# Reordering loads, splits and GpSimd's sums in a graph-attention and top-p diffusion kernel

## Chip, cores and metric

The kernel runs on one core of a Trainium2 chip. A core has five instruction queues that run beside each other: TensorE (PE, matrix products), VectorE (DVE), ScalarE (ACT), GpSimd (POOL) and SyncE (SP, which here only starts transfers). The metric is the time of one execution on the device in microseconds (us).

## What is computed

Two layers over N = 4096 nodes with D = 256 features, each with a layer norm and a relu ahead of it and the input added behind it. The first is a graph attention with 4 heads. The second runs two steps: in each, a softmax over all nodes is cut to the smallest set of largest probabilities that reaches 0.9 of the sum, and used as one neighbour matrix; a normalised adjacency is the other. Cut to what matters:

```python
# layer 0
h   = relu(layernorm(x))
e   = leaky_relu(src[:, :, None] + dst.T[None])       # src, dst: h @ W, then a
out = einsum('nhm,mhd->nhd', softmax(where(adj > 0, e, -9e15)), h @ W)
x   = x + layernorm(out) * gamma + beta
# layer 1
X   = relu(layernorm(x));  R = adj + I;  R = R / R.sum(-1)
Xf = Xa = X;  Z = 0
for n in range(2):
    p  = softmax((Xa @ W1.T @ W2.T) @ (Xa @ W3.T).T)
    A  = p * (p is among the largest that reach 0.9);  A = A / A.sum(-1)
    Xf = R @ Xf
    Xa = A @ Xa
    Z  = Z + Xf @ U1[n].T + Xa @ U2[n].T
x   = x + layernorm(X + Z) * ln_g + ln_b
```

## The kernel before

Nodes are cut into NB = 32 blocks of P = 128. The stages follow each other: a prologue (features of layer 0), layer 0's attention in 16 passes, the first graph hop (R @ Xf), attention step 0, a "join" (second graph hop, with projections for step 1 between its products), attention step 1, and a tail. Except in layer 0's passes the order on each engine is the order in which the program calls its functions (`manual_schedule`); there a scheduler places instructions within the order of dependences. [...]

**Prologue.** SP loads X (block 0, blocks 1 to 3, then four at a time), ScalarE's queue starts the loads of a_r (L198) and of the weights wx in two halves (L200). VectorE makes two columns per head out of wx and a_r (L545, L547), and each block is normalised, turned and multiplied.

**Layer 0.** A pass k is a group of 8 blocks of rows and one head; 16 pairs p of column blocks run through it. VectorE makes masks m (L375, L376), TensorE multiplies (L395). Work that belongs to an earlier pass is put into a list `later`, from which one piece is taken for each pair. Lifted sums (L578) add beta to X on GpSimd in the passes of head 0. For the first hop, `source`, `split` (L450 on ScalarE, L451 on VectorE: a row block in two parts, high and low), `edge` (load of an adjacency strip `ar`, or `aru` for every fifth) and `own` (L602: the identity added to it) prepare the first strips.

**Hops.** `hops` goes through strips n: source, edge, split, own, then the products L615. `drained` copies four sums out (L626), ScalarE and VectorE taking two each. Between step 0 and step 1, Xa is loaded back into X in eight loads, one at each sixth half step.

**Attention.** A block b has three parts: logits and exponentials two or three blocks ahead (L720, L903), the search for its threshold, and `attend`, which turns its kept probabilities (L1080, copied out by L1082) and multiplies them with X (L1088) in eight groups g of four. At the end of `attend`, L1098 multiplies by U1 and L1102 on ScalarE writes the result into xf. The search needs sums from ScalarE (L910); `first_step` on GpSimd makes of them a first limit c3 in 17 small instructions (L927 to L953); `third_probe` (L971) on VectorE uses it on the whole row, then eight-maxima (L989, L996) give the threshold, and `masked` (L1014) clears what is below.

`chosen_kept(b)` puts these in order for each block, together with the last layer norm, which only step 1 has:

- `gathered(b-1)`, GpSimd: part + v, x1 + ln_b, part + xf (L1106 to L1108). The last needs L1102.
- `finish(b-2)`, VectorE: adds the scaled sum (L1269), mean and variance (L149, L150).
- `finish_scale(b-2)`, GpSimd: rs and nmr (L1276, L1277, L1280).
- `normal(b-2)`, ScalarE: part times rs plus nmr (L1284). It comes last in `chosen_kept`, so on ScalarE it stands right behind L1102 of the block before and ahead of L903 of the next.
- `polished(b-3)`, GpSimd: times ln_g, plus x1 (L1288, L1289), and the store (L1290, SP).

The first three blocks of a step get their `first_step` in the stage before it.

**Repair.** Rows whose threshold wasn't settled are counted (`questioned`, up to L1168 on VectorE; `counted`, two matmuls L870), and a branch (L1256) behind the last block redoes blocks where there are any. `looked` does the count, `number` reads it into registers of all engines.

Of the kernel before, what the change touches and what calls it, by code (L numbers as in the profile page):

```python
# [56 lines left out]
def gat_then_top_p_diffusion(  # L57
# [104 lines left out]
    with tc.tile_pool(name="l0", bufs=1) as l0, tc.tile_pool(name="l0s", bufs=2) as l0s, tc.tile_pool(name="l0o", bufs=1) as l0o:  # L162
# [26 lines left out]
        with tc.manual_schedule(engines=every | {ET.SP}):  # L189
# [5 lines left out]
                nc.sync.dma_start(X[:, ts(g, 4), :], x[ts(g, 4 * P), :].rearrange("(b p) d -> p b d", p=P))  # L195

            nc.sync.dma_start(X[:, 0, :], x[:P, :])
            nc.scalar.dma_start(a_r, bass.AP(tensor=a.tensor, offset=a.offset, ap=[[0, P], [1, 2 * HD]]))  # L198
            for k in range(KC):
                nc.scalar.dma_start(wx[:, k, :D], w[ts(k, P), :])  # L200
            nc.sync.dma_start(X[:, 1:4, :], x[P:4 * P, :].rearrange("(b p) d -> p b d", p=P))
            for g in range(1, NB // 4):
                block_rows(g)
# [195 lines left out]
        def evacuate(k):  # L399
            ig, h = passes[k]  # L400
            acc = shared[k].acc
            if h == 0:
                out_rows[ig] = l0o.tile([P, G0, D], F32, name="o")
            st = l0o.tile([P, 4, 2 * H * (W3 + 1) // 2], F32, name="st").rearrange("p a b -> p (a b)")
            st = st[:, :G0 * 2 * W3].rearrange("p (i t k d) -> p i t k d", i=G0, t=2, k=3)
            for i in range(G0):
                b = ig * G0 + i
                one, two = (st[:, i, t].rearrange("p k d -> p (k d)") for t in range(2))
                nc.scalar.activation(two, acc[i][:, 1, :W3], AF.Copy, scale=e_c[1][:, h, b:b + 1])
                if h == 0:  # L410
                    nc.vector.reduce_sum(rinv[:, b:b + 1], acc[i][:, :, W3], axis=AX.X)
                nc.vector.scalar_tensor_tensor(one, acc[i][:, 0, :W3], e_c[0][:, h, b:b + 1], two, ALU.mult, ALU.add)

            def three():
                for n in (1, 2):
                    nc.vector.tensor_tensor(st[:, :, 0, 0], st[:, :, 0, 0], st[:, :, 0, n], ALU.add)

            def divided():
                rden = small.tile([P, G0], F32, name="rden")
                nc.vector.reciprocal(rden, st[:, :, 0, 0, HD])  # L420
                nc.vector.tensor_mul(out_rows[ig][:, :, ts(h, HD)], st[:, :, 0, 0, :HD],
                                     rden[:, :, None].to_broadcast([P, G0, HD]))
                if h == 0:
                    rs = rinv[:, ts(ig, G0)]
                    nc.vector.tensor_scalar(rs, rs, 1.0, None, ALU.add)
                    nc.vector.reciprocal(rs, rs)
            return [three, divided] + (closing(ig) if h == H - 1 else [])

        PASSES = NB // G0
        S = SimpleNamespace(spare=None)  # L430
# [15 lines left out]
        def split(A, n):  # L446
            while A.parted < min(n, len(order)):
                src = A.src[A.parted]
                hl = rp.tile([P, 2, D], F32R, name="hl", bufs=5)
                nc.scalar.copy(hl[:, 0, :], src)  # L450
                nc.vector.tensor_tensor(hl[:, 1, :], src, hl[:, 0, :].bitcast(F32), ALU.subtract)  # L451
                A.hl[A.parted] = hl
                A.parted += 1

        hop1 = hop_of(0)

        def closing(ig):
            o = out_rows[ig]
            mv = l0s.tile([P, G0, nc.vector.BN_AGGR_DIM], F32, name="mv8")
            scales = []  # L460

            def stats(i0):
                for i in range(i0, i0 + 2):
                    moments_of(mv[:, i, :], o[:, i, :])
                if i0 == G0 - 2:
                    scales.extend(steps(mv, G0, l0s))

            def close(i):
                b = ig * G0 + i
                xb = X[:, b, :]  # L470
                ob = l0s.tile([P, D], F32, name="ob")
                nc.scalar.activation(ob, o[:, i, :], AF.Identity, scale=scales[0][:, i:i + 1], bias=scales[1][:, i:i + 1])
                nc.vector.tensor_mul(ob, ob, gamma_r)
                nc.vector.tensor_add(xb, xb, ob)
                nc.sync.dma_start(x1_d[b], xb)
                moments_of(mv[:, i, :], xb)
                if i == G0 - 1:
                    steps(mv, G0, l0s, x_rs[:, ts(ig, G0)], x_nmr[:, ts(ig, G0)])

            def relu(i0):  # L480
                for b in range(ig * G0 + i0, ig * G0 + i0 + 2):
                    nc.scalar.activation(X[:, b, :], X[:, b, :], AF.Relu, scale=x_rs[:, b:b + 1], bias=x_nmr[:, b:b + 1])
                if ig == 0 and i0 < LOOK + 1:
                    for b in range(i0, min(i0 + 2, LOOK + 1)):
                        source(hop1, b)
                        split(hop1, b + 1)
            return [lambda i=i: stats(i) for i in range(0, G0, 2)] + [lambda i=i: close(i) for i in range(G0)] \
                + [lambda i=i: relu(i) for i in range(0, G0, 2)]

# [50 lines left out]
        with tc.manual_schedule(engines=every):  # L540
# [22 lines left out]
            for n, (k, p) in enumerate(todo):  # L563
# [9 lines left out]
                    products(k, p, ms.pop(n))  # L573
                if n in rest:
                    rest[n]()
                if k % H == 0 and 2 < p < PAIRS - 1 and lifted:
                    b = lifted.pop(0)
                    nc.gpsimd.tensor_tensor(X[:, b, :], X[:, b, :], beta_r, ALU.add)  # L578
                if 1 < p < PAIRS - 3 and later:
# [3 lines left out]
        passing.close()  # L583
        ps2 = ctx.enter_context(tc.tile_pool(name="ps2b", bufs=2, space=PSUM))
        ps1 = ctx.enter_context(tc.tile_pool(name="ps1b", bufs=2, space=PSUM))
        def edge(A, n):
            if n in A.ar or n >= len(order):
                return
            p, j = order[n]
            if S.spare is not None and n % 5 == 4:  # L590
                ar = S.spare.tile([P, G0 * P], F32R, name="aru", tag="u")
            else:
                ar = rp.tile([P, G0 * P], F32R, name="ar", bufs=4)
            nc.sync.dma_start(ar.bitcast(F32), adj_d[p, :, j, :].bitcast(F32))
            A.ar[n] = ar

        def own(A, n):
            while A.owned < min(n, len(order)):
                p, j = order[A.owned]
                if j // G0 == p:  # L600
                    block_ = A.ar[A.owned][:, ts(j % G0, P)]
                    nc.vector.tensor_tensor(block_, block_.bitcast(F32), ident, ALU.add)  # L602
                A.owned += 1

        def graph_products(A, m, s, halves=(0, 1)):
            j = order[m][1]
            if j == 0 and s == 0:
# [10 lines left out]
        def drained(hop, p, acc):  # L618
# [2 lines left out]
            room = S.big if last else S.l1e.tile([P, N], F32, name="stage", tag="e1")  # L621
            out_ = room[:, :N // 2].rearrange("p (c s b i) -> p c s b i", c=2, s=KC, b=4)
            rows_ = room[:, ds(N // 2, N // 2)].rearrange("p (b d) -> p b d", b=G0)
            for c in (1, 0):
                for s in range(KC):
                    (nc.vector.tensor_copy if s else nc.scalar.copy)(out_[:, c, s].rearrange("p b i -> p (b i)"), acc[c][s])  # L626

            def stored():
                for c in range(2):
# [25 lines left out]
        def hops(A):  # L655

            turned = []
            for n in range(A.begun, len(order) + LOOK + 1):
                for i in range(3 if n == A.begun else 1):
                    source(A, n + 2 - (2 - i if n == A.begun else 0))  # L660
                edge(A, n)
# [677 lines left out]
    for n in range(STEPS):  # L1339
# [4 lines left out]
        with tc.manual_schedule(engines=every):  # L1344
# [1 line left out]
            filling, picking = fills(n, G, found, blocks), picks(n, found, blocks)  # L1346
            done = 0 if n else NB - G0 - LOOK
            for i, _ in enumerate(pieces, 2 * done):
                if n > 0 and i % 6 == 5 and i // 6 < NB // 4:
                    g = i // 6  # L1350
                    nc.sync.dma_start(cur[:, ts(g, 4), :], xa_d[ts(g, 4)].rearrange("b p d -> p b d"))
                if (n == 0 or i > 10) and i // 2 % NB != NB - 2:
# [11 lines left out]
            def chosen_kept(b):  # L1364

                r = blocks[b]
                if not hasattr(r, "kept"):
                    candidates(r, found)
                if b > 2:
                    polished(blocks.pop(b - 3))  # L1370
                if b + 1 < NB and not hasattr(blocks[b + 1], "thirded"):
                    third_probe(blocks[b + 1])
                if b > 1:
                    finish(blocks[b - 2])
                    finish_scale(blocks[b - 2])
                if b + 2 < NB and not hasattr(blocks[b + 2], "stepped"):
                    first_step(blocks[b + 2])
                if 0 < b < NB - 1:
                    gathered(blocks[b - 1])
                if not hasattr(r, "kept"):  # L1380
                    masked(r)
                if 1 < b < NB - 1:
# [12 lines left out]
            def beginning():  # L1395
                normal(blocks[NB - 3])
                gathered(blocks[NB - 2])
                finish(blocks[NB - 2])
                finish_scale(blocks[NB - 2])
                R.count = number(R, R.undone)  # L1400

            beside = {NB - 2: {5: last_chosen, 6: looked}, 0: dict(zip((0, 1, 3, 5, 6), S.turned))}
            for b in range(NB - 1):
                chosen_kept(b)
                if b + AHEAD < NB:
# [6 lines left out]
                polished(blocks[NB - 3])  # L1412
                finish_rows(blocks[NB - 2])

            beside = {0: beginning, 3: earlier}
            if n + 1 < STEPS:
                second = hop_of(n + 1)
                beside.update({1: both_weights, 2: lambda: begin(second, 4), 5: lambda: split(second, 2), 6: lambda: (split(second, 4), own(second, 4))})
            attend(r, cur, None, beside)
            for m in range(second.begun if n + 1 < STEPS else 0):  # L1420
                for s in range(KC):
# [37 lines left out]
```

## Time and profile before

| | |
|---|---|
| median of three runs | 2875.74 us (2874.88 to 2879.38) |
| the profiled execution | 2872.68 us, span 2870.9 us |
| busy: TensorE, VectorE, ScalarE, GpSimd | 2798.5, 2169.1, 1919.1, 867.1 us |
| mean granted TensorE clock | 0.994 |
| layer 0's passes | some 89 to 797 us |
| first hop | to 1120 us |
| attention step 0, with its last block | to 1806 us |
| join | to 2165 us |
| attention step 1, tail | to 2845 us, to 2871 us |

The profile comes from one execution. A line of a timeline gives start and duration in us, engine, line of the program, operation, output and inputs with their shapes, and in brackets how long the engine had been idle and what released it. A line of waits gives who waited for what: us in total, times, the longest. A line of a stretch gives its ends and length, then busy time (and instructions) of PE, PE's weight loads, DVE, ACT and POOL, granted clock, share of the DMA engines and GB/s.

### The profile page before, as it was taken

How to read it: one execution, taken by the hardware profiler on the slowest of the kernel's cores; microseconds unless marked ns; L12 is line 12 of the kernel's file. 1: busy time of each engine (PE TensorE's matmuls, PEld its weight loads, DVE VectorE, ACT ScalarE, POOL GpSimd, SP SyncE). 2: the span in 40 equal slices, each digit the busy share in tenths (PEclk: the TensorE clock that was granted, in tenths of full speed). 3: DMA queues.
4: the chain of work that ended last, by engine and by line, in shares of the span. 5: the costliest groups of instructions: out<-in, count | busy, mean ns of one | idle time of the engine just before them, and what ended most of it. 6: DMA issues, size and time to landing. Idle time of an engine off the chain costs nothing. (4 is left out here: it accounts for less than half of the span.)

```text
span 2870.9 us, 51480 instructions
## 1 busy us (share of the span) xinstructions
PE 2798.5 (97%) x18777; PEld 2440.2 (85%) x18777; DVE 2169.1 (76%) x5069; ACT 1919.1 (67%) x3065; POOL 867.1 (30%) x1811
## 2 busy tenths in 40 slices
PE   5899999999999999999999999999999999999998
PEld 4899999999987788888888888667878888888887
DVE  8867878678654385888888887343574999999996
ACT  7876887779633646788777884232627778877882
POOL 6501211110000121322332221000204766666564
PEclk9999999999999999999999999999999999999999
DMA  8969587696366783000000001667991111111100
GB/s 193 243 229 222 186 232 186 242 194 226 141 227 199 237 296 104 20 20 20 24 23 20 20 20 48 217 205 234 326 349 49 31 34 39 31 31 31 41 29 25
DMA packets 190394, 376.48 MB, mean 131 GB/s; under 512 B 18224, under 2 KB 143152, under 8 KB 186032
## 3 DMA queue, kind: packets, MB, share of 16 engines
q1 hardware_dynamic: 146832, 275.05, 28.9%
q0 software_dynamic: 21504, 83.89, 12.3%
q10 hardware_dynamic: 21792, 14.11, 1.5%
q8 instruction: 152, 2.49, 0.3%
q14 instruction: 114, 0.93, 0.1%
HBM read 305.55 MB, written 113.57 MB: 146 GB/s over the span
## 5 line engine op out<-in xcount | busy, mean ns | idle before, releaser
L1088 PE MATMUL acc<-X,eT 128*128 128x256 f32 x4096 | 973.8, 383 | 3.4 <-ACT eT L1082 2.8
L1088 PEld LDWEIGHTS acc<-X,eT 128*128 128x128 f32 x4096 | 739.9, 191 | 110.5 <-ACT eT L1082 31.4
L395 PE MATMUL acc<-ut,m 128*128 128x195 bf16 (+1 forms) x8192 | 699.5, 247 | 7.0 <-DVE m L376 4.9
L395 PEld LDWEIGHTS <-m 128*128 128x128 fp8e4 x8192 | 696.1, 96 | 10.3 <-DVE m L376 6.1
L369 ACT ACTIVATE g<-sr,d_big 128x1024 uint8<-128x1024 f32 x448 | 472.8, 1136 | 6.4 <-DVE m L375 6.3
L903 ACT ACTIVATE e<-mm,nm 128x1024 f32<-128x1024 f32 x256 | 286.1, 1117 | 201.5 <-PE mm L720 197.8
L1082 ACT COPY eT<-tp 128x512 f32<-128x512 f32 x512 | 296.4, 580 | 89.5 <-PE tp L1080 89.2
L989 DVE MAX8 cand<-big 128x8 f32<-128x228 f32 (+1 forms) x1152 | 348.3, 380 | 0.0
L615 PE MATMUL mm<-ar,hl 128*128 128x512 f32 x844 | 342.7, 409 | 5.5 <-DMA ar<-adj_d 1.6
L971 DVE SCALAR_TENSOR_TENSOR big<-e,c 128x4096 f32<-128x4096 f32 x58 | 261.9, 4516 | 97.9 <-POOL c L956 67.1
L615 PE MATMUL acc<-ar,hl 128*128 128x512 f32 x844 | 329.2, 393 | 0.4 <-DVE ar L602 0.4
L927 POOL TENSOR_TENSOR sums<-sums 128x2 f32<-128x2 f32 x64 | 12.8, 200 | 1033.4 <-ACT void L910 1033.4
L1080 PE MATMUL tp<-ident,e 128*128 128x128 f32 x2048 | 306.3, 273 | 0.8 <-DVE e L1014 0.8
L1080 PEld LDWEIGHTS tp<-ident,e 128*128 128x128 f32 x2048 | 255.0, 141 | 60.2 <-PE acc L1098 1.2
L1014 DVE SCALAR_TENSOR_TENSOR e<-e,found 128x4096 f32<-128x4096 f32 x58 | 259.1, 4468 | 0.0
L375 DVE TENSOR_TENSOR m<-g,ax 128x512 uint32<-128x512 uint32 x256 | 179.5, 701 | 104.6 <-PE acc L395 92.4
L910 ACT ACTIVATE void<-e,c1x 128x2048 int8<-128x2048 f32 x128 | 257.4, 2011 | 0.9 <-DMA ar<-adj_d 0.5
L910 ACT ACTIVATE void<-e,c 128x2048 int8<-128x2048 f32 x128 | 257.4, 2011 | 0.0
L720 PE MATMUL mm<-kT,qT 128*128 128x512 f32 x512 | 198.5, 469 | 3.6 <-ACT e L903 1.9
L376 DVE TENSOR_TENSOR m<-m,ax 128x512 uint32<-128x512 uint32 x256 | 180.5, 705 | 25.9 <-DVE m L375 0.5
L615 PEld LDWEIGHTS mm<-ar,hl 128*128 128x128 f32 x844 | 159.5, 189 | 45.8 <-issue 6.9
L615 PEld LDWEIGHTS acc<-ar,hl 128*128 128x128 f32 x844 | 159.6, 189 | 36.8 <-issue 4.1
(302 smaller groups left out, 3512.3 us busy)
## 6 DMA issues: line engine op xcount, KB each, us to landing
ar<-adj_d SPq DMA_DIRECT2D x211, 512.0 KB, 4.5
adj_d<-ax POOLq DMA_DIRECT2D x32, 2048.0 KB, 7.5
ut<-uv_d SPq DMA_DIRECT2D x60, 784.0 KB, 5.6
aru<-adj_d SPq DMA_DIRECT2D x45, 512.0 KB, 4.5
ax<-in_adj_t_dram POOLq DMA_DIRECT2D x32, 512.0 KB, 17.5
x<-xf_d SPq DMA_DIRECT2D x78, 128.0 KB, 4.8
xf<-xft_d SPq DMA_DIRECT2D x64, 128.0 KB, 2.2
sr<-s_d SPq DMA_DIRECT2D x15, 512.0 KB, 4.8
```

What stands on the lines that cost most here:

```text
L369: nc.scalar.activation(g[:, c, :], shared[k].sr, AF.Relu, scale=BIG, bias=d_big[:, h, j:j + 1])
L395: nc.tensor.matmul(shared[k].acc[i][:, t, :cols], m[t][:, c, ts(i, P)], shared[k].ut[j // QUARTER][:, j % QUARTER, t, :cols], start=(j == ...
L615: nc.tensor.matmul(A.acc[c][s], A.hl[m][:, t, ts(s, P)], A.ar[m][:, ts(c, 512)], start=(j == 0 and t == 0), stop=(j == NB - 1 and t == 1))
L720: nc.tensor.matmul(pm[:, h, :], q[t], kT[:, ds(h * (N // 2) + c * 512, 512)], start=(t == 0), stop=(t == 1))
L903: nc.scalar.activation(ev[:, :, c, :], r.pm[c], AF.Exp, bias=r.nm, accum_out=r.sums[:, c // 2, c % 2:c % 2 + 1])
L910: nc.scalar.activation(void, r.e[:, ts(h, N // 2)], (AF.Relu, AF.Sign)[i], bias=r.c1, scale=-1.0, accum_out=r.sums[:, h, 2 + i:3 + i])
L971: nc.vector.scalar_tensor_tensor(big, r.e, r.c3, r.e, ALU.is_le, ALU.mult, accum_out=r.low3)
L989: nc.vector.max(cand[:, s, :], big[:, edges[s]:edges[s + 1]])
L1014: nc.vector.scalar_tensor_tensor(r.e, r.e, r.t, r.e, ALU.is_ge, ALU.mult, accum_out=kept)
L1080: nc.tensor.transpose(pt[:, i, :], r.e[:, ts(4 * g + i, P)], ident)
L1082: nc.scalar.copy(eT, pt)
L1088: nc.tensor.matmul(r.acc[:, 0, :], eT[:, i, :], cur[:, j, :], start=(j == 0), stop=(j == NB - 1))
```

## The change

1. Prologue: a_r's load and both of wx are issued by SP, between X's block 0 and blocks 1 to 3.
2. Layer 0: the first hop's splits, edges and own sums become pieces of `later` in passes 6, 7 and 10. In pass 0, the lifted sums begin at pair 8, not 3.
3. `drained`: the four copies in another order.
4. Join: the first edge that isn't begun yet is issued ahead of the sources; X's loads come at half step 1 of six, not 5.
5. `chosen_kept`: on GpSimd gathered, polished, first_step, finish_scale in place of polished, finish_scale, first_step, gathered.
6. Repair: the count moves from group 6 of the last block but one to group 1 of the last block; it is read at group 4, not 0; the weights U2 are loaded at group 2, not 1.

```diff
             nc.sync.dma_start(X[:, 0, :], x[:P, :])
-            nc.scalar.dma_start(a_r, bass.AP(tensor=a.tensor, offset=a.offset, ap=[[0, P], [1, 2 * HD]]))
+            nc.sync.dma_start(a_r, bass.AP(tensor=a.tensor, offset=a.offset, ap=[[0, P], [1, 2 * HD]]))
             for k in range(KC):
-                nc.scalar.dma_start(wx[:, k, :D], w[ts(k, P), :])
+                nc.sync.dma_start(wx[:, k, :D], w[ts(k, P), :])
...
-            return [three, divided] + (closing(ig) if h == H - 1 else [])
+            def sourced(n):
+                source(hop1, n)
+                split(hop1, n + 1)
+
+            ready = []
+            if k == H + 1:
+                ready = [lambda n=n: sourced(n) for n in range(LOOK + 1)]
+            elif k == H + 2:
+                ready = [lambda n=n: edge(hop1, n) for n in range(LOOK)]
+            elif k == 2 * H + 1:
+                ready = [lambda n=n: own(hop1, n + 1) for n in range(LOOK)]
+            return [three, divided] + ready + (closing(ig) if h == H - 1 else [])
...
-                if ig == 0 and i0 < LOOK + 1:
-                    for b in range(i0, min(i0 + 2, LOOK + 1)):
-                        source(hop1, b)
-                        split(hop1, b + 1)
...
-                if k % H == 0 and 2 < p < PAIRS - 1 and lifted:
+                if k % H == 0 and (2 if k else 7) < p < PAIRS - 1 and lifted:
...
-            for c in (1, 0):
-                for s in range(KC):
-                    (nc.vector.tensor_copy if s else nc.scalar.copy)(out_[:, c, s].rearrange("p b i -> p (b i)"), acc[c][s])
+            for c, s in ((1, 0), (0, 0), (0, 1), (1, 1)):
+                (nc.vector.tensor_copy if s else nc.scalar.copy)(out_[:, c, s].rearrange("p b i -> p (b i)"), acc[c][s])
...
             for n in range(A.begun, len(order) + LOOK + 1):
+                if n == A.begun:
+                    edge(A, n)
...
-                if n > 0 and i % 6 == 5 and i // 6 < NB // 4:
+                if n > 0 and i % 6 == 1 and i // 6 < NB // 4:
...
                 if not hasattr(r, "kept"):
                     candidates(r, found)
+                if 0 < b < NB - 1:
+                    gathered(blocks[b - 1])
                 if b > 2:
                     polished(blocks.pop(b - 3))
+                if b + 2 < NB and not hasattr(blocks[b + 2], "stepped"):
+                    first_step(blocks[b + 2])
                 if b + 1 < NB and not hasattr(blocks[b + 1], "thirded"):
                     third_probe(blocks[b + 1])
                 if b > 1:
                     finish(blocks[b - 2])
                     finish_scale(blocks[b - 2])
-                if b + 2 < NB and not hasattr(blocks[b + 2], "stepped"):
-                    first_step(blocks[b + 2])
-                if 0 < b < NB - 1:
-                    gathered(blocks[b - 1])
...
+            def asked():
                 R.count = number(R, R.undone)
 
-            beside = {NB - 2: {5: last_chosen, 6: looked}, 0: dict(zip((0, 1, 3, 5, 6), S.turned))}
+            beside = {NB - 2: {5: last_chosen}, 0: dict(zip((0, 1, 3, 5, 6), S.turned))}
...
-            beside = {0: beginning, 3: earlier}
+            beside = {0: beginning, 1: looked, 3: earlier, 4: asked}
...
-                beside.update({1: both_weights, 2: lambda: begin(second, 4), 5: lambda: split(second, 2), 6: lambda: (split(second, 4), own(second, 4))})
+                beside.update({2: lambda: (both_weights(), begin(second, 4)), 5: lambda: split(second, 2), 6: lambda: (split(second, 4), own(second, 4))})
```

`edge` and `own` are also moved, unchanged, from behind the passes to ahead of `hop1`.

More of the change, by code (lines that the diff above doesn't have):

```diff
@@ L453, in split, with edge, own @@
                 A.parted += 1
+        def edge(A, n):
+            if n in A.ar or n >= len(order):
+                return
+            p, j = order[n]
+            if S.spare is not None and n % 5 == 4:
+                ar = S.spare.tile([P, G0 * P], F32R, name="aru", tag="u")
+            else:
+                ar = rp.tile([P, G0 * P], F32R, name="ar", bufs=4)
+            nc.sync.dma_start(ar.bitcast(F32), adj_d[p, :, j, :].bitcast(F32))
+            A.ar[n] = ar
+        def own(A, n):
+            while A.owned < min(n, len(order)):
+                p, j = order[A.owned]
+                if j // G0 == p:
+                    block_ = A.ar[A.owned][:, ts(j % G0, P)]
+                    nc.vector.tensor_tensor(block_, block_.bitcast(F32), ident, ALU.add)
+                A.owned += 1
         hop1 = hop_of(0)
@@ L585, in gat_then_top_p_diffusion @@
         ps1 = ctx.enter_context(tc.tile_pool(name="ps1b", bufs=2, space=PSUM))
[L586 to L603, printed above, removed]
         def graph_products(A, m, s, halves=(0, 1)):
```

## The prediction

> **What bounds it now.** I read the busy shares, then the stretch of attention step 1 by itself, then its waits, then its engines in order of time. Line numbers are those of the kernel before.
>
> ```profile
> PE 2798.5 (97%) x18777; PEld 2440.2 (85%) x18777; DVE 2169.1 (76%) x5069; ACT 1919.1 (67%) x3065; POOL 867.1 (30%) x1811
> DVE 18%; PE 12%; issue 5%; DMA 1%; ACT 1%; POOL 0%; SPq 0%; POOLq 0%; ACTq 0%; DVEq 0%
> ```
>
> TensorE is busy 97%; the chain of waits (second line) leans to VectorE, so the stretch must decide. Engine busy times of 2165 to 2845 us:
>
> ```profile
> 2165.00:2845.00 680.00, 675.88 (x3526) 577.50 (x3525) 634.55 (x1511) 518.64 (x820) 425.36 (x733) 1.00 0.11 32
> ```
>
> TensorE works 675.88 of 680 us, VectorE (third) 634.55, ScalarE 518.64, GpSimd 425.36. The waits of 2230 to 2800 us list no wait of a matmul, so TensorE bounds step 1, at 22.26 us a block (L1102 at 2601.60 and at 2623.87). Next, where GpSimd stands against ScalarE at a block's border. GpSimd:
>
> ```profile
> 2594.82 4.36 POOL L1276 TENSOR_SCALAR rs<-mv 128x1 f32<-128x1 f32 x1 [6.12 <-DVE mv L150]
> 2599.93 0.26 POOL L1280 TENSOR_SCALAR nmr<-mv,rs 128x1 f32<-128x1 f32 x1
> 2600.73 0.19 POOL L927 TENSOR_TENSOR sums<-sums 128x2 f32<-128x2 f32 x1 [0.55 <-ACT void L910]
> ...
> 2607.03 0.34 POOL L953 TENSOR_SCALAR c<-fell,c,up 128x1 f32<-128x1 f32 x1
> 2607.33 0.73 POOL L1106 TENSOR_TENSOR part<-part,xa 128x256 f32<-128x256 f32 x1
> ...
> 2608.70 0.73 POOL L1108 TENSOR_TENSOR part<-part,xf 128x256 f32<-128x256 f32 x1
> ...
> 2610.21 0.73 POOL L1289 TENSOR_TENSOR part<-part,x 128x256 f32<-128x256 f32 x1
> ```
>
> ScalarE, and then TensorE, at that border:
>
> ```profile
> 2601.60 0.47 ACT L1102 ACTIVATE xf<-acc,rinv 128x256 f32<-128x256 f32 x1 [0.95 <-PE acc L1098]
> 2601.98 0.59 ACT L1284 ACTIVATE part<-part,nmr,rs 128x256 f32<-128x256 f32 x1
> 2602.53 1.12 ACT L903 ACTIVATE e<-mm,nm 128x1024 f32<-128x1024 f32 x1
> ```
>
> ```profile
> 2604.27 1.99 PE L1088 MATMUL acc<-X,eT 128*128 128x256 f32 x8
> ```
>
> ScalarE runs L1102 (xf of the block just ended), L1284 (normal, which needs nmr of L1280), L903, then the copy eT, for which L1088 waits. Today nmr is out at 2600.19, before L1284, so nothing waits.
>
> [...] L1276 takes 4.36 us beside L1014, 0.22 free; at 2185 L1107 (0.73 elsewhere) waits out L971:
>
> ```profile
> 2184.24 0.34 POOL L953 TENSOR_SCALAR c<-fell,c,up 128x1 f32<-128x1 f32 x1
> 2184.56 0.73 POOL L1106 TENSOR_TENSOR part<-part,xa 128x256 f32<-128x256 f32 x1
> 2185.24 4.91 POOL L1107 TENSOR_TENSOR x<-x,ln_b_r 128x256 f32<-128x256 f32 x1
> ```
>
> ```profile
> 2184.62 4.95 DVE L971 SCALAR_TENSOR_TENSOR big<-e,c 128x4096 f32<-128x4096 f32 x1 [26.79 <-POOL c L953]
> ```
>
> [...] L1284 waits there and TensorE behind it; after the pause, eight L1088 take 3.49 us, not 1.89.
>
> ```profile
> 2822.78 0.60 ACT L1284 ACTIVATE part<-part,nmr,rs 128x256 f32<-128x256 f32 x1 [1.26 <-POOL nmr L1280]
> ```
>
> ```profile
> 2823.90 3.49 PE L1088 MATMUL acc<-X,eT 128*128 128x256 f32 x8 [1.03 <-ACT eT L1082]
> ```
>
> **GpSimd's order, the part that decides.** In step 1 a block's GpSimd work was polished (L1288, L1289), finish_scale (L1276 to L1280), first_step (L927 to L953), gathered (L1106 to L1108). It becomes gathered, polished, first_step, finish_scale. ScalarE's order is unchanged: L1102, L1284, L903. The position of each instruction in the two programs shows no other change in step 1. So L1108 of gathered waits for L1102, all else on GpSimd queues behind it, and L1284, the very next instruction on ScalarE, needs the last of that queue. Nothing of it can start before L1102, and TensorE gets no eT until it is through. With t the end of L1102:
>
> - L1108, L1288, L1289: 2.24 us from start to start (2608.70 to 2610.94). first_step: 6.60 (2600.73 to 2607.33). L1276 starts at t + 8.9.
> - L953's c3 releases L971. VectorE's work is 634.55 / 680 of 22.26 = 20.8 us a block, so in a longer period it sits there waiting, as at 2184[...]. L1276 (0.22) slips in; L1277 is held 4.4 us and L1280 follows: nmr at t + 14.5. Without the collision the three take 1.2 us: t + 10.1.
> - From L1284's start to L1088: 2.29. From L1088 to the next L1102: 19.60, and 0.47 to its end. The restart at half clock costs 3.49 - 1.89 = 1.6, taken as 1.7.
> - Period: 14.5 + 2.3 + 19.6 + 0.5 + 1.7 = 38.6, that is +16.3 us on 22.26. Uncollided: 34.2, +11.9.
>
> First_step here and normal both run for blocks 2 to 29: 28 x 16.3 = **+456 us**. Block 30 has no first_step, about +3; in exchange VectorE is no longer late at the tail (0.80 and 1.03 us of waits and the 1.6 above): -3.5. Step 0 has no gathered, polished or normal work, so nothing there. What SP issues for it, polished's store (L1290), now waits until t + 2.3 with the next block's loads behind it; those are used 19 us later, so hidden. VectorE also gains: its L1001, L1005, L1006 (0.68, 0.59, 0.79 us) ran beside the 128x256 sums and take 0.32, 0.19, 0.27 in step 0. That 1.3 us a block isn't on the path: TensorE has no wait for it.
>
> **The other parts**, all small.
> - Prologue: a_r and both wx loads go ahead of the bulk X loads on SP. VectorE waited 2.99 us for wx until 7.72. The loads are 1 instruction and 2; X[1:4] behind them is issued about 1.4 us later, needed at 9.30. **-2.4** (-3.5 to 0).
> - Layer 0: hop 1's splits go from one burst at 332 to 343, where TensorE stands 0.54 + 1.06 + 0.54, to one a pair; L602 leaves the place where VectorE waits 3.88 us for a load and TensorE 2.7; five L578 sums leave the start-up, where TensorE stands 0.87. These are most of the 6.0 us below. The moved work costs VectorE the same anywhere, and it is 74% busy there (526 of 708), so it has room: **-5** (-7 to 0). The ar loads stand where they did on SP.
>
> ```profile
> PE acc L395 <- DVE m L376: 4.9, 5, 2.7
> PE acc L395 <- DVE m L375: 1.1, 1, 1.1
> ```
>
> - L626 copies: only VectorE's two swap places; TensorE waits 0.9 on them: 0 (-1 to +1).
> - Join: edge 4 is issued ahead of its sources, and X's loads four half steps earlier. Waits of 1.85 (aru) and 1.93 (X); the next ar, pushed back by one X load, may be late by up to 1.4: **-2.4** (-4 to +1).
> - Repair: the count's matmuls L870 leave the end of block 30, where they wait 1.26 (step 0) and 1.64 us (tail) for L1168; the value is read at g = 4, both_weights one group later. L1168 is then long done: -2.9. New is that every engine reads the count at g = 4, three groups (3 x 2.17 us by L1088's starts in the tail) behind the matmuls; the count's own VectorE steps lie between, and if they are late TensorE stands too. I keep 1.2 for that: **-1.7** (-2.9 to +2). The two u2 loads of both_weights go to SP 2.2 us later and are used only in the join.
>
> Sum: 456 + 3 - 3.5 - 2.4 - 5 - 2.4 - 1.7 = +444 on the profiled execution's 2872.68: 3317. The median of the runs is 3.1 above that: **3320 us**.
>
> **Rivals.**
> - No collision ([...]VectorE a little late at L971): 28 x 11.9 = 333, so 3197. For it: L1276 to L1280 take 1.2 us when free. Against: 2184. Chance 0.17.
> - A second collision: [...]L1280 comes after L1014 has started (1.08 us behind L971's end) and is held 4.4 more: +123, so 3443. At 2190, GpSimd went on at once when L971 ended, so 0.09.
> - Faster: L1284's wait is hidden. It needs nmr before L1102 ends, that is GpSimd 14.5 us earlier, so a gathered that doesn't depend on that L1102, or a normal that ScalarE reaches that much later. Then only the small parts count, -11.5: 2864. The program order of both engines speaks against it: 0.04.
> - The reorder changes less than I read, or its pieces cancel: 0.01 for no difference.
>
> The likeliest case has 0.69: with 15 to 17.7 us a block it lies at 3280 to 3360. To hold 8 in 10 the range goes down to the uncollided case with its bounds, 3185, and up to 3375; the second collision stays out. Faster by over 0.2% (5.8 us, about what a measurement here can tell) 0.04, within 0.01, slower 0.95.
>
> **What would show it.** Right: L1284 idle some 14 us a block for nmr, GpSimd's L1277 at 4.9 us beside L971, TensorE near 60% busy in step 1 with a granted clock below 1, a period near 38.6, other stages nearly unchanged. L1277 at 0.57: the uncollided case. Wrong: L1284 without a wait in step 1.

## The result, and the profile after

| | before | after |
|---|---|---|
| median | 2875.31 us (4 runs, 2873.13 to 2879.38) | 3345.82 us (4 runs, 3343.13 to 3348.28) |
| profiled execution, span | 2872.68, 2870.9 us | 3347.00, 3345.1 us |
| granted TensorE clock | 0.994 | 0.930 |

The ratio is 1.1636, with a 95% interval of 1.1619 to 1.1652: the changed kernel is 16% slower. The forecast was 3320 us, in a range of 3185 to 3375. In step 1 and the tail a line number of the changed file is 8 higher than before (L1102 is now L1110, L1284 is L1292, L1276 is L1284).

The page of the changed kernel, busy shares and the chain of waits:

```profile
PE 2865.8 (86%) x18777; PEld 2485.7 (74%) x18777; DVE 2133.7 (64%) x5069; ACT 1920.8 (57%) x3065; POOL 983.2 (29%) x1811
issue 19%; PE 13%; POOL 10%; ACT 2%; DVE 1%; DMA 1%; SPq 0%; POOLq 0%; DVEq 0%; ACTq 0%
```

In the second line, "issue" is time in which nothing that the profile shows held the engine. TensorE falls from 97% to 86% of a longer span. GpSimd, 0% of the chain before, is 10% of it now. The blocks 2 to 29 of step 1, as one stretch:

```profile
2193.00:3288.00 1095.00, 685.74 (x3232) 576.22 (x3231) 574.22 (x1440) 485.29 (x766) 517.62 (x698) 0.80 0.06 18
```

TensorE is busy 685.74 of 1095 us (63%), at a granted clock of 0.80 instead of 1.00. No engine is full: the engines wait for each other. The waits of the same stretch (total, times, longest):

```profile
DVE big L979 <- POOL c L961: 497.9, 28, 18.9
...
PE acc L1096 <- ACT eT L1090: 409.3, 28, 15.4
ACT part L1292 <- DVE mv L150: 204.9, 14, 14.7
ACT part L1292 <- POOL nmr L1288: 203.7, 14, 14.7
```

TensorE waits 28 times for eT, ScalarE 28 times in L1292. Half of ScalarE's waits are put down to L150 only because the L150 of the next block happens to end with nmr (both at 2717.81 in the block below); it isn't the L150 that nmr is made from, since L1284, which reads that one's result, starts at 2712.30. One border between two blocks, GpSimd first:

```profile
2703.34 0.73 POOL L1116 TENSOR_TENSOR part<-part,xf 128x256 f32<-128x256 f32 x1 [19.65 <-issue]
...
2711.87 0.34 POOL L961 TENSOR_SCALAR c<-fell,c,up 128x1 f32<-128x1 f32 x1
2712.30 4.51 POOL L1284 TENSOR_SCALAR rs<-mv 128x1 f32<-128x1 f32 x1
...
2717.55 0.26 POOL L1288 TENSOR_SCALAR nmr<-mv,rs 128x1 f32<-128x1 f32 x1
2717.77 5.00 POOL L1114 TENSOR_TENSOR part<-part,xa 128x256 f32<-128x256 f32 x1
```

VectorE, ScalarE and TensorE at the same border:

```profile
2712.25 4.49 DVE L979 SCALAR_TENSOR_TENSOR big<-e,c 128x4096 f32<-128x4096 f32 x1 [18.72 <-POOL c L961]
```

```profile
2702.74 0.47 ACT L1110 ACTIVATE xf<-acc,rinv 128x256 f32<-128x256 f32 x1 [0.96 <-PE acc L1106]
2717.85 0.60 ACT L1292 ACTIVATE part<-part,nmr,rs 128x256 f32<-128x256 f32 x1 [14.64 <-DVE mv L150]
2718.36 1.10 ACT L911 ACTIVATE e<-mm,nm 128x1024 f32<-128x1024 f32 x1
```

```profile
2720.07 3.78 PE L1096 MATMUL acc<-X,eT 128*128 128x256 f32 x8 [14.63 <-ACT eT L1090]
```

L1110 ends at 2703.21 and releases L1116; the bracket of L1116 names no releaser, but it starts 0.13 us behind the end of L1110 in every one of these blocks. GpSimd then goes through polished and first_step. c3 (L961) lets VectorE into L979, whose 4.49 us hold GpSimd's L1284 for 4.51 (0.21 us in experiment 5, where it comes ahead of c3). nmr is out 14.6 us after L1110; until then ScalarE stands at L1292, and L911 and the copy L1090, for which TensorE waits, stand behind it.

The small parts show where they should. The masks' waits in layer 0 (6.0 us before) are down to 0.2:

```profile
PE acc L395 <- DVE st L412: 1.7, 2, 1.0
...
PE acc L395 <- DVE m L376: 0.2, 1, 0.2
```

### The profile page after: what moved, and what is told of

Its sections match the earlier page's. It is cut to its first block, busy times and chain, and to the rows that moved or that the text cites. A ratio compares the mean times of both kernels' runs of the same rounds, so it can differ in the third digit from the quotient of the medians.

```text
span 3345.1 us, 51496 instructions
## 1 busy us (share of the span) xinstructions
PE 2865.8 (86%) x18777; PEld 2485.7 (74%) x18777; DVE 2133.7 (64%) x5069; ACT 1920.8 (57%) x3065; POOL 983.2 (29%) x1811
## 5 line engine op out<-in xcount | busy, mean ns | idle before, releaser
L1096 PE MATMUL acc<-X,eT 128*128 128x256 f32 x4096 | 1024.6, 397 | 419.7 <-ACT eT L1090 419.2
L1096 PEld LDWEIGHTS acc<-X,eT 128*128 128x128 f32 x4096 | 770.8, 198 | 540.0 <-ACT eT L1090 449.0
L979 DVE SCALAR_TENSOR_TENSOR big<-e,c 128x4096 f32<-128x4096 f32 x58 | 260.6, 4493 | 593.7 <-POOL c L961 526.3
L911 ACT ACTIVATE e<-mm,nm 128x1024 f32<-128x1024 f32 x256 | 285.5, 1115 | 264.3 <-PE mm L728 262.2
L1090 ACT COPY eT<-tp 128x512 f32<-128x512 f32 x512 | 296.7, 581 | 95.3 <-PE tp L1088 95.2
L1088 PE MATMUL tp<-ident,e 128*128 128x128 f32 x2048 | 311.5, 276 | 1.0 <-DVE ns_i_u L884 1.0
L1088 PEld LDWEIGHTS tp<-ident,e 128*128 128x128 f32 x2048 | 260.9, 143 | 62.7 <-issue 3.2
L1022 DVE SCALAR_TENSOR_TENSOR e<-e,found 128x4096 f32<-128x4096 f32 x58 | 259.1, 4468 | 0.0
L1292 ACT ACTIVATE part<-part,nmr,rs 128x256 f32<-128x256 f32 x30 | 18.0, 601 | 416.4 <-POOL nmr L1288 211.4
L728 PE MATMUL mm<-kT,qT 128*128 128x512 f32 x512 | 209.8, 492 | 3.2 <-ACT e L911 2.2
L1116 POOL TENSOR_TENSOR part<-part,xf 128x256 f32<-128x256 f32 x32 | 23.4, 730 | 589.5 <-issue 589.5
```

Source lines behind the costliest of these rows:

```text
L728: nc.tensor.matmul(pm[:, h, :], q[t], kT[:, ds(h * (N // 2) + c * 512, 512)], start=(t == 0), stop=(t == 1))
L911: nc.scalar.activation(ev[:, :, c, :], r.pm[c], AF.Exp, bias=r.nm, accum_out=r.sums[:, c // 2, c % 2:c % 2 + 1])
L979: nc.vector.scalar_tensor_tensor(big, r.e, r.c3, r.e, ALU.is_le, ALU.mult, accum_out=r.low3)
L1022: nc.vector.scalar_tensor_tensor(r.e, r.e, r.t, r.e, ALU.is_ge, ALU.mult, accum_out=kept)
L1088: nc.tensor.transpose(pt[:, i, :], r.e[:, ts(4 * g + i, P)], ident)
L1090: nc.scalar.copy(eT, pt)
```

## Experiments

**Theory:** ScalarE stands in normal, in program order ahead of all it does for the next block, until GpSimd has gone through gathered, polished, first_step and a finish_scale that VectorE's L979 holds up. **Rivals:** VectorE, idle 18.7 us a block for a late c3, is what holds the period; another part of the change costs the time; the collision is no real cost. A "period" is the time from one L1110 to the next. In the edits below the lines with `if` are left out; where it helps, a comment gives the condition.

**1. The order alone.** The kernel before, with this edit and no other:

```diff
+                gathered(blocks[b - 1])                 # 0 < b < NB - 1
                 polished(blocks.pop(b - 3))
+                first_step(blocks[b + 2])
                 third_probe(blocks[b + 1])
                 finish(blocks[b - 2])
                 finish_scale(blocks[b - 2])
-                first_step(blocks[b + 2])
-                gathered(blocks[b - 1])
```

> The kernel before with nothing but the new order in chosen_kept (gathered, polished, first_step, finish_scale). Theory (ScalarE stands at normal until GpSimd has gone through all of it): the whole loss is here. 28 blocks at 17.0 us more, as in the changed kernel, and 5 to 7 at its end: 2875 + 482 = about 3357, that is some 10 us above the changed kernel, which also has the small gains. Rival (another part of the change takes a share, for instance the later count or the loads): clearly under 3330.

Measured: 3348.88 us, ratio 1.1658 (1.1624 to 1.1692). The whole loss is in the order. It is 8 us under the expected 3357. Against the runs of before that were taken beside it (2872.40) it is 476.5 us slower, where 482 were expected.

**2. All but the order.** The changed kernel, with chosen_kept as it was (the edit above turned round).

> The changed kernel with chosen_kept's order of before; all other parts stay. Theory: gains of the small parts as the trace of the changed kernel has them, 7.5 us up to the end of layer 0 and 0.5 after it, and about 1 at the tail: 2866 to 2868. Rival by my sum (each small part worth what was forecast, 11.5): 2864. Rival (late count and changed loads cost in step 1 what they gain before): 2873 to 2878.

Measured: 2861.73 us against 2873.96 of the runs of before taken beside it, ratio 0.9961 (0.9947 to 0.9975). The other parts together gain 12.2 us; the forecast had 11.5. The expectation, 2866 to 2868, was too slow by 4 us or more: it put the gain at about 9. In the trace 8.9 us are gained up to step 1 and 2.5 at its end.

**3. finish_scale ahead of first_step.** The changed kernel, with this edit:

```diff
                 polished(blocks.pop(b - 3))
-                first_step(blocks[b + 2])
                 third_probe(blocks[b + 1])
                 finish(blocks[b - 2])
                 finish_scale(blocks[b - 2])
+                first_step(blocks[b + 2])
```

> The changed kernel with finish_scale ahead of first_step again: gathered, polished, finish_scale, first_step. Theory: nmr comes 2.3 + 1.2 = 3.5 us behind L1102's end, so TensorE stands 3.5 us a block, with 0 to 1.7 for the clock: period 25.8 to 27.5, total 2966 to 3014. No collision: VectorE isn't in L979 or L1022 then. Rival (VectorE's late limit c3, which comes at t + 10.1 here, later than in the changed kernel, is what holds the block): 3340 or more.

Measured: 3016.49 us, 2.5 above the upper end; ratio 1.0501 (1.0471 to 1.0532). Against the rival: c3 comes later here than in the changed kernel (L961 at 2614.76, 9.9 us after the end of L1110, against 8.7), and still 329 us of the loss are gone. ScalarE's line at a border:

```profile
2608.54 0.60 ACT L1292 ACTIVATE part<-part,nmr,rs 128x256 f32<-128x256 f32 x1 [3.72 <-POOL nmr L1288]
```

**4. gathered last.** The changed kernel with gathered behind finish_scale, so that first_step doesn't wait for L1110:

```diff
-                gathered(blocks[b - 1])
                 polished(blocks.pop(b - 3))
                 first_step(blocks[b + 2])
                 third_probe(blocks[b + 1])
                 finish(blocks[b - 2])
                 finish_scale(blocks[b - 2])
+                gathered(blocks[b - 1])
```

> The changed kernel with gathered behind the rest again: polished, first_step, finish_scale, gathered. first_step then waits for ScalarE's sums, 1.3 us ahead of L1102, not for L1102. Theory with collision: c3 at t + 5.3, L979 at once, the three of finish_scale done at about t + 10.5, period about 35, total near 3225. Theory without collision: nmr at t + 6.5, period about 30, total near 3090. Rival (gathered's wait for L1102 is the whole of it): within 30 of 2870.

Measured: 3223.45 us, ratio 1.1222 (1.1189 to 1.1254), the case with a collision. So gathered ahead of the rest isn't the whole of it: finish_scale behind first_step alone makes nmr 10.9 us late. GpSimd, and then ScalarE:

```profile
2620.30 4.51 POOL L1284 TENSOR_SCALAR rs<-mv 128x1 f32<-128x1 f32 x1
```

```profile
2625.86 0.60 ACT L1292 ACTIVATE part<-part,nmr,rs 128x256 f32<-128x256 f32 x1 [10.94 <-POOL nmr L1288]
```

**5. The collision taken away.** The changed kernel, with finish_scale called from within first_step just ahead of its last two instructions, those that make c3. The GpSimd instructions are the same, but their order isn't: finish_scale also comes ahead of two instructions of first_step, which take 1.1 us (2711.20 to 2712.30 in the changed kernel).

```diff
+        ahead()                      # finish_scale(blocks[b - 2])
         c3, t = col("c3", 6), col("fell", 2)
         pool.tensor_tensor(t, inv_e, y, ALU.pow)
         pool.tensor_scalar(c3, t, r.c1, up, ALU.mult, ALU.mult)
```

> The changed kernel with finish_scale's three instructions put ahead of the last two of first_step, so that they are issued before c3 lets VectorE into L979. Same GpSimd work in the same place, but for the collision. Theory with collision: nmr at t + 9.1 rather than t + 14.6, 5.5 us less a block, 28 blocks: 3346 - 154 = about 3192. Rival (4.4 us of L1284 beside L979 is an artefact of the profile, or hidden): 3320 to 3350.

Measured: 3198.80 us, ratio 1.1136 (1.1103 to 1.1168), 147 us under the changed kernel and 7 above the expectation. nmr comes 9.33 us behind L1110 and not 14.65. Of these 5.3 us, 1.1 are the two instructions; 4.2 are the collision, about what L1284 is held for (4.51 us against 0.21). That is some 118 of the 147 us. The three small instructions take 1.2 us when VectorE isn't in L979 (GpSimd, then ScalarE; lines are one higher in this file):

```profile
2608.70 0.21 POOL L1285 TENSOR_SCALAR rs<-mv 128x1 f32<-128x1 f32 x1
2608.99 0.56 POOL L1286 TENSOR_TENSOR rs<-rs,mhalf 128x1 f32<-128x1 f32 x1
2609.65 0.26 POOL L1289 TENSOR_SCALAR nmr<-mv,rs 128x1 f32<-128x1 f32 x1
```

```profile
2609.95 0.60 ACT L1293 ACTIVATE part<-part,nmr,rs 128x256 f32<-128x256 f32 x1 [9.33 <-POOL nmr L1289]
```

**6. ScalarE a block later.** The changed kernel, GpSimd's order as changed; only ScalarE's normal moves:

```diff
                 gathered(blocks[b - 1])
+                normal(blocks[b - 3])                   # b > 2
                 polished(blocks.pop(b - 3))
...
-                normal(blocks[b - 2])                   # 1 < b < NB - 1
```

> The changed kernel, GpSimd's order as changed, but ScalarE's normal for block b - 3 (not b - 2) in chosen_kept(b), ahead of polished(b - 3). GpSimd is as slow as before and c3 as late (about t + 9.6), only ScalarE doesn't stand for nmr of the same block. Theory: ScalarE's L1292 waits for nothing, period 22.3 to 22.8, total 2867 to 2885. Rival (VectorE, idle 18.7 us a block for c3, is what holds the period): stays within 10% of 3346.

Measured: 2858.56 us, ratio 0.9947 (0.9932 to 0.9963). That is 8 us below the expected 2867 to 2885. The loss is gone with GpSimd as slow as in the changed kernel, and the rival falls. GpSimd, VectorE and ScalarE at a border:

```profile
2600.46 4.51 POOL L1284 TENSOR_SCALAR rs<-mv 128x1 f32<-128x1 f32 x1
```

```profile
2600.41 4.48 DVE L979 SCALAR_TENSOR_TENSOR big<-e,c 128x4096 f32<-128x4096 f32 x1 [1.21 <-POOL c L961]
```

```profile
2590.80 0.47 ACT L1110 ACTIVATE xf<-acc,rinv 128x256 f32<-128x256 f32 x1 [0.96 <-PE acc L1106]
2591.17 0.59 ACT L1292 ACTIVATE part<-part,nmr,rs 128x256 f32<-128x256 f32 x1
...
2613.06 0.47 ACT L1110 ACTIVATE xf<-acc,rinv 128x256 f32<-128x256 f32 x1 [0.96 <-PE acc L1106]
```

The collision is there, VectorE even waits 1.21 us for c3, and the period is 22.26 us, because L1292 finds an nmr that is a block old. This version and number 2 both beat the kernel before, by 0.5 and 0.4%. It is 3.2 us faster than number 2 on the same chip, with ranges that don't overlap (2857.7 to 2859.75 and 2861.24 to 2864.33). Their blocks of step 1 have the same period; the traces put 2 us of it into the join, which this edit doesn't touch, and 1 into the tail. What makes that difference is open.

**7 and 8. An array that isn't let idle.** The changed kernel, with matmuls put into TensorE's wait whose result is overwritten later; 56 a block, and then 30:

```diff
+            if g == 0 and r.n + 1 == STEPS and 1 < r.b < NB - 1:
+                for _ in range(56):
+                    nc.tensor.matmul(r.far, X[:, r.b, :P], X[:, r.b, :], start=True, stop=True)
             gather(r, eT[g], g, cur)
```

> The changed kernel with 56 more matmuls a block (13.2 us at 0.236) into a part of PSUM that is overwritten later, put where TensorE waits 14.6 us for eT; for blocks 2 to 30. Theory: they run inside the wait and the array is at full clock when the real work starts again, so the first eight L1096 take 1.9 to 2.0 us, not 3.78, and each period loses 1.7 (forecast) to 2.7 (the longer of the two periods): 3346 - 48 to 76, 3270 to 3298. Rival (the restart at half clock costs nothing outside those eight, or something else makes every second period 1 us longer): 3346 or, if the matmuls reach beyond the wait, more.

Measured: 3553.17 us, ratio 1.2364 (1.2341 to 1.2386). A miss: I had taken an entry of the trace for a matmul, and each makes two. 56 took 24.34 us and reached beyond the wait, so they were the bound:

```profile
2701.74 24.34 PE L1139 MATMUL acc<-X 128*128 128x256 f32 x112
```

> As the run with 56 added matmuls a block, with 30: that run's trace shows that one takes 0.434 us (two passes), so 56 took 24.3 us and reached 9.7 us beyond the wait of 14.6; 30 take 13.0. Theory: the array is at full clock when the real work starts, the first four L1096 (eight passes) take 1.9 to 2.0 us and not 3.78, and the pairs of 38.75 and 39.77 us become even, at 22.25 + 14.6 = 36.9: 3346 - 28 x 2.4 = about 3279. Rival (the second, longer period has another cause, and the restart costs only the 1.8 us of the first four): half of the periods stay 1 us longer, 3346 - 28 x 1.8 = 3296.

Measured: 3284.05 us, ratio 1.1421 (1.1399 to 1.1443), clock 0.996. Everything waits as before (nmr 14.60 us), but the first matmuls after the wait are at full speed, and the period is an even 36.88 us (L1110 at 2712.24 and 2749.12):

```profile
2714.77 13.12 PE L1139 MATMUL acc<-X 128*128 128x256 f32 x60
2729.54 1.99 PE L1096 MATMUL acc<-X,eT 128*128 128x256 f32 x8 [1.65 <-ACT eT L1090]
```

So the restart at half clock costs 39.26 - 36.89 = 2.37 us a block (means of 26 blocks), and the lower clock is a small part of the loss: with a clock of 0.996 the kernel is still 14% slower than before.

**9. Without the late count.** Number 2, with the count of the repair where it was before ("..." stands for the rest of the line):

```diff
-            beside = {NB - 2: {5: last_chosen}, 0: ...}
+            beside = {NB - 2: {5: last_chosen, 6: looked}, 0: ...}
-            beside = {0: beginning, 1: looked, 3: earlier, 4: asked}
+            beside = {0: beginning, 3: earlier}
```

In this run the count is also read at group 0 and U2 loaded at group 1, as before.

> All parts but the order in chosen_kept, and without the late count either (count at group 6 of the last block but one, read at group 0, U2 at group 1). Theory from the stages of the run with all but the order: the late count is worth 0.8 us at the end of step 0 and about 2.7 at the tail, so 2862 + 3.5 = about 2865. By my forecast (1.7): 2863.5. Rival (the new waits at the later read eat it): 2861 to 2862.

Measured: 2865.49 us, ratio 0.9965 (0.9951 to 0.9979). That is 3.8 us above number 2, but in another set of runs, and the two ratios differ by less than either interval: the timing doesn't settle it. The trace of this run shows where a gain would lie:

```profile
2833.26 0.22 PE L878 MATMUL tp<-undone,ones 128*1 128x32 f32 x2 [3.32 <-DVE undone L1176]
```

With the late count those two matmuls wait for nothing and L1088 behind them 0.55 us for the count's VectorE steps. From block 29's L1110 to the end, run 9 takes 51.5 us, number 2 47.3 and the kernel before 49.9, in one trace of each.

## Why the prediction was right

**GpSimd's order.** For blocks 2 to 29 right in each step, except for which instruction collides (below), and the wait is right in size: the periods of six runs, by how late nmr is after L1110.

| run | wait of L1292, us | mean period, us | period less 22.25 and the wait | half of the half-clock time behind the wait, us |
|---|---|---|---|---|
| 6, normal a block later | 0 | 22.25 | 0.0 | 0 |
| 3, finish_scale ahead of first_step | 3.8 | 27.84 | 1.8 | 1.9 |
| 5, no collision | 9.3 | 34.13 | 2.5 | 2.6 |
| 4, gathered last | 10.9 | 35.27 | 2.1 | 2.1 |
| the changed kernel | 14.6 | 39.26 | 2.4 | 2.4 |
| 8, the array kept busy | 14.6 | 36.89 | 0.0 | 0 |

Means are over blocks 3 to 28; 22.25 is the period before. Each microsecond of ScalarE's wait is a microsecond of the period; the rest is the restart, and with the array kept busy it is nil. The last column comes from the granted clock in the traces: the time for which it is still 0.5 after the matmuls have started again, halved. In runs 1, 3, 4, 5 and the changed kernel it gives the rest of each single one of 130 periods to within 0.11 us.

Forecast was +16.3 a block (38.6), measured +17.0. Of its terms, nmr at t + 14.5 (14.6), 2.3 from L1292 to TensorE (2.2) and the 4.4 us for which VectorE holds GpSimd (4.3) held. The one that was mis-sized is the restart at half clock: taken as 1.7 from one stall in the tail of before, where half clock lasted 3.41 us, it is 2.4 on average, because here half clock outlasts the wait by 3.7 and 5.9 us in turn. 28 blocks came to +475 instead of +456.

**Which instruction collides.** Forecast was that L1276 (now L1284) slips in and L1277 is held. L979 started 0.05 us ahead of L1284, which was held instead. The price is the same: my sums gave 123 us for it in all (28 times 38.6 less 34.2), and of the 147 us of experiment 5 some 118 are the collision.

**The end of step 1.** Forecast 3 - 3.5. Measured: block 30 takes 30.0 us instead of 24.3 and block 31 one more, +6.7 together. The step that failed is block 30's, where I saw no collision because it has no first_step; there VectorE's L1022 (4.65 us from 3290.91) holds L1284:

```profile
3291.38 4.27 POOL L1284 TENSOR_SCALAR rs<-mv 128x1 f32<-128x1 f32 x1
```

**The small parts**, by the stages of the two traces:

| part | forecast, us | changed kernel, us |
|---|---|---|
| prologue (first L254 at 12.0, was 13.9) | -2.4 | -1.9 |
| layer 0 (its last product, beyond the prologue) | -5 | -5.6 |
| first hop | 0 | +1.5 |
| late count in step 0 | part of -1.7 | -0.4 |
| join | -2.4 | -1.5 |

One trace doesn't settle a microsecond or two here: run 1, whose stages up to step 1 are those of before, reaches the end of layer 0 1.7 us and step 1 2.9 us earlier than the profile of before. The gain of prologue and layer 0 together is clear of that (6.7 to 7.6 us in the nine traces with the change). The first hop was forecast at nothing and gives back 1.5 (0.2 to 1.9 in the nine); its waits are spread over a dozen lines of about 1 us each, and I did not find one that makes it. In step 0 the count's wait of 1.26 us is gone and one of 0.49 came at the later read. In the join, X's wait is gone as forecast and a new one came (1.27 us for L482, the identity added to the early strip), with 0.58 for the next ar:

```profile
1806.26 0.50 PE L622 MATMUL acc<-aru,hl 128*128 128x512 f32 x1 [1.27 <-DVE aru L482]
1811.67 0.47 PE L622 MATMUL mm<-ar,hl 128*128 128x512 f32 x1 [0.58 <-DMA ar<-adj_d]
```

The join's gain isn't steady: 1.5 us in the changed kernel and in run 2, 3.8 in run 6, 4.2 in run 9, but a loss of 1.4 in run 8, and run 1 has 1.1 us of it without the change; its size stays open. Forecast for the late count at the tail was 1.64 us less a new wait; with before's order (runs 2 and 9) the trace shows 3.32 us turned into 0.55. In the profile of before, 1.64 stood there, because the restart at half clock just ahead had already used up the rest: TensorE was early for L1168 either way. L1168 ends 21.03 us after the start of block 29's L1102 in the profile of before, and the same instruction as long after it in run 9. So the 1.6 us of restart in my -3.5 were never on the path.

Sum: +475 + 6.7 - 8.0 (up to step 1's block 2) = +474 on the profiled execution, where the forecast had +444. Of the 30 us between them 19 are the restart, 7 the last two blocks, 4 the small parts. That the small parts of run 2 fit so well as a sum (12.2 against 11.5) is in part luck: the first hop and the join gave less than forecast, the tail more.

**The rivals.** No collision (3197): experiment 5 gives 3199 when the collision is taken away, and that it fits to 2 us is luck. Its nmr came at 9.3 and not at the 10.1 of the rival, because two instructions stood behind it, and its restart cost 2.5 and not 1.7. The faster one (2864) is what experiment 6 gives, 2859, when ScalarE reaches normal a block later: the condition named for it. The second collision (3443) did not come, but it was near: L1288 starts at 2717.55, 0.18 us ahead of L1022.

## What to carry to other kernels

Before a producer is moved behind something, find the instruction that waits for it and read what is queued behind that instruction on its engine: an off-path result of 1.2 us of work, asked for early on ScalarE with L911 and L1090 behind it, cost 17 us a block here. When an order has to change, move the consumer with the producer: normal one block later made the same GpSimd order free. A new order that makes an engine wait also moves the start of its work, which can then meet work that it never met before: VectorE, once it waited for c3, started L979 0.03 us behind the end of L961 in all 28 blocks, just ahead of the next instruction of GpSimd, which had made c3.

## What the runs showed of the hardware

- ScalarE kept the program's order through the wait. At the border shown above TensorE stood from 2705.44 on, so L911's product was out by then, but L911 started at 2718.36, 0.51 us behind the start of L1292. It is 0.50 or 0.51 us in all 27 blocks that have both.
- Where VectorE's L979 and a GpSimd instruction followed c3 together, the one that started first ran freely, even if it was less than 0.1 us ahead. In all 28 blocks of the changed kernel L979 started 0.05 us ahead (2712.25, L1284 at 2712.30): L979 took 4.49 us and L1284, 0.21 when free, 4.51. At a border of run 3 GpSimd's L1114 started 0.08 us ahead (2615.06, L979 at 2615.14): L1114 took 0.73 us and L979 4.93.
- The granted clock changed at times of its own, not at the pause. In the traces of before and of the changed kernel it changes 15 and 71 times, always at a whole number of steps of 3.413 us from the first record of it. In the changed kernel half clock begins 3.5 and 4.7 us behind the start of TensorE's pause in turn and lasts 5 and 4 steps, and so periods with the same wait alternate, 38.75 and 39.77 us, 23 steps for two. In run 5 every period is 10 steps, 34.13 us; in run 4 three periods (34.64, 36.03 and 35.14 us) make 31. With the array kept busy (run 8) all periods are 36.89. Two stretches of half clock in the changed kernel (the granted clock is the 0.50); TensorE's busy time in them, 3.69 and 5.92 us, all lies behind the wait:

```profile
2710.11:2723.76 13.65, 3.69 (x9) 2.97 (x10) 11.41 (x13) 3.75 (x7) 12.70 (x10) 0.50 0.03 10
2747.66:2764.73 17.07, 5.92 (x16) 4.71 (x16) 13.65 (x21) 4.14 (x8) 13.68 (x13) 0.50 0.08 25
```

- Two short pauses close together were followed by half clock in one of two cases: 0.80 and 1.03 us in the profile of before (3.49 us for the next eight matmuls, granted clock 0.50 from 2824.23 to 2827.64), but not 0.84 and 1.04 in run 2 (1.99 us). In the 3.4 us ahead of 2824.23 TensorE was busy for 1.57 us, so it had not been idle for a whole step. Two cases don't show what decides it.
